# Layer 0's cross-attention: the reciprocals of the softmax sums taken one step later, behind the first four maxima of that step

## The chip, the cores and the metric

One NeuronCore of a Trainium2 chip runs the whole program. The metric is device time in microseconds (us): the kernel before takes 3111.43 us, the median of three runs that lie between 3109.09 and 3111.95. A core has five engines that work side by side, each through its own queue in order: PE (TensorE, matmuls; its weight loads are listed apart as PEld), DVE (VectorE), ACT (ScalarE), POOL (GpSimd) and SP (SyncE, which here only starts DMAs). They wait for each other through semaphores.

## The reference, cut to what matters

The program is a two-layer decoder on 32 sequences of 100 tokens with 256 channels. Each layer adds a self-attention, a cross-attention and a feed-forward block with experts. The change lies in layer 0's cross-attention, with 16 heads of 16 channels and 361 context rows per sequence:

```python
Q = (x @ Wq.T).reshape(B, xN, NUM_HEADS, HEAD_DIM)
KV = (z @ Wkv.T).reshape(B, zN, 2, NUM_HEADS, HEAD_DIM)
...
attn = jnp.einsum('bqhd,bkhd->bhqk', Q, K) * SCALE
attn = jax.nn.softmax(attn, axis=-1)
O = jnp.einsum('bhqk,bkhd->bqhd', attn, V).reshape(B, xN, DIM)
return O @ Wo.T
```

All of it is float32. A softmax needs a maximum over the 361 scores of a row, exponentials, their sum, and a division by that sum; the division is done on the output, after the product with V.

## The kernel before, in words

The function is `l0_xattn` (L513). Its work is cut into 64 units: unit M is sequence b = M // 2 and half c = M % 2 of the heads, thus 8 heads. Eight heads of 16 channels are laid on 128 partitions as four groups of 32 rows (r = 0 to 3), and each group holds two heads (j = 0 and 1), which are taken one after the other. The loop at L717 runs 66 steps; step M works on three units at once, in a software pipeline:

- `maxima(M-1)` (L618): PE turns the row maxima of the unit before (two transposes, L623), DVE adds them to the queries (L625). The tile is q2. An extra row of ones in the keys (L583) lets the next matmul subtract the maximum.
- `scores(M, j)` (L607): four matmuls with 100 queries as rows, one per group, into four PSUM banks; then four DVE maxima (L616), one per bank.
- `turned(M-1, j)` (L627): the same scores again, turned (context rows on partitions) and with the maximum subtracted: 12 matmuls into four banks, four exponentials on ACT (L637, tile e), and two additions on POOL (L641, L642, tile es), which fold the three context chunks into one, so that fewer matmuls are needed for the sum.
- `values(M-2)` (L644): 24 matmuls with V (L651) and 8 with ones (L658) into one bank, which then holds the products and the sums. ACT copies the bank to the tile zs (L663), DVE takes the reciprocal of the sums in place (L664, 128x100), POOL multiplies (L666) into zT, the input of the output projection.
- the extras of the step (L685): keys (L583) and values (L592) of the next sequence, whose PSUM banks ACT copies out (L588, L601); at every second step (c = 1) of two sequences in four also queries (L574, copies L581); at most steps with c = 0 an output projection `out_proj` (L237), whose result DVE adds to x (L243) and takes statistics of (L179, L182); and, at certain steps, pieces for the feed-forward block that follows: normalised rows on DVE (L191), their transposes (L213), and the router's logits and choice (`gates0`, L1428, with DVE's sums at L1449; `counts0`, L1453).

Inside step M the order for j = 0 is scores, turned, values, then for j = 1 scores and turned, then the extras. PE's order is exactly the written one (`manual_schedule`, L707); the queues of the other engines are ordered by the framework's scheduler.

All PSUM tiles of this function come from one ring of eight banks (`bank`, L111: every tag falls back to "t", of which there are eight). The ninth tile from any point gets the bank of the first, so a matmul waits until the reader of the tile eight places before it is done. In one step the ring is handed out as: 1 (maxima), 4 (scores j = 0), 4 (turned j = 0), 1 (values), 4 (scores j = 1), 4 (turned j = 1), then the extras, first among them the keys. Counting back eight from the keys' bank gives the first bank of scores j = 1: the keys' matmul waits for the first of the second four maxima. Counting back from turned j = 0 of the next step gives the banks of turned j = 1, of the extras and of the maxima's transposes: it waits for ACT's copies of keys, values and queries.

DVE's queue in a plain step holds: q2 (L625), four maxima of j = 0, the reciprocal of unit M-2, four maxima of j = 1.

The inner functions `scores` and `values`, and the loop that calls them, are printed here with the profile's line numbers:

Of the kernel before, what the change touches and what calls it, by code (L numbers as in the profile page):

```python
# [13 lines left out]
ALU = mybir.AluOpType  # L14
AX = mybir.AxisListType
# [66 lines left out]
class Kernel:  # L82
# [430 lines left out]
    def l0_xattn(self):  # L513
        nc, tc, a = self.nc, self.tc, self.a
        with ExitStack() as st:
# [54 lines left out]
            def load(b):  # L570
                ctx[b] = pool.tile([CD, LP], F32, tag="cT", name="cT", bufs=3)
                nc.sync.dma_start(ctx[b], a["ctxT"][:, b, :])

            def queries(b0, c):  # L574
                if c == 0:
                    q[b0 // 4] = pool.tile([P, 2, 2, 4 * T], F32, tag="qT", name="qT")
                pm = self.bank_t()[:, : 4 * T]
                self.mm(pm, [(wq[:, k, c * P : (c + 1) * P], self.xn_of(k, b0, 4)) for k in range(NK)])
                t = q[b0 // 4]
                for j in range(2):  # L580
                    nc.scalar.activation(t[:, c, j, :], pm, AF.Copy, scale=quarter[:, j : j + 1])  # L581

            def keys(b, c):  # L583
                pm = self.bank_t()[:, :L]
                self.mm(pm, [(wk[:, c * P : (c + 1) * P], ctx[b][:, :L])])
                t = ks[b % 3]
                for j in range(2):
                    nc.scalar.activation(  # L588
                        t[:, c, j, :L], pm, AF.Identity, bias=one[:, j : j + 1], scale=own[:, j : j + 1]
                    )  # L590

            def vals(b, c0, n):  # L592
                pm = self.bank_t()[:KC, : n * D].rearrange("p (c d) -> p c d", c=n)
                for i in range(n):
                    c = c0 + i
                    self.mm(pm[:, i, :], [(ctx[b][:, c * KC : (c + 1) * KC], wv)])
                pv = pm.rearrange("p c (h j d) -> p c h j d", j=2, d=16)
                v = vs[b % 3][:, c0 : c0 + n].rearrange("p c (h j) e -> p c h j e", j=2)
                for j in range(2):
                    for i in range(n):  # L600
                        nc.scalar.copy(v[:, i, :, j, 16 * j : 16 * j + 16], pv[:, i, :, j, :])  # L601

            def rows_of(r):
                return slice(32 * r, 32 * r + 32)


            def scores(M, j):  # L607
                b, c = divmod(M, 2)
                cols = slice((b % 4) * T, (b % 4 + 1) * T)
                ps = [self.bank("r")[:T, :L] for _ in range(4)]  # L610
                for r in range(4):
                    self.mm(ps[r], [(q[b // 4][rows_of(r), c, j, cols], ks[b % 3][rows_of(r), c, j, :L])])
                m = ms[M % 3]
                for r in range(4):
                    o = 32 * r + 16 * (1 - j)
                    nc.vector.tensor_reduce(m[:, j, o : o + 1], ps[r], AX.X, ALU.max, negate=True)  # L616

            def maxima(M):  # L618
                b, c = divmod(M, 2)
                cols = slice((b % 4) * T, (b % 4 + 1) * T)  # L620
                pt = self.bank_t()[:, : 2 * T].rearrange("p (j t) -> p j t", j=2)
                for j in range(2):
                    nc.tensor.transpose(pt[:, j, :], ms[M % 3][:, j, :], self.ident[:T, :T])  # L623
                q2[M] = pool.tile([P, 2, T], F32, tag="q2", name="q2")
                self.after = nc.vector.tensor_tensor(q2[M], pt, q[b // 4][:, c, :, cols], ALU.add)  # L625

            def turned(M, j):  # L627
                b, c = divmod(M, 2)
                ps = [self.bank("r")[:KC, : NKC * T] for _ in range(4)]
                for i in range(NKC):  # L630
                    for r in range(4):
                        self.mm(ps[r][:, i * T : (i + 1) * T], [(
                            ks[b % 3][rows_of(r), c, j, i * KC : (i + 1) * KC], q2[M][rows_of(r), j, :]
                        )])
                t = e[M, j] = pool.tile([KC, 4, NKC, T], F32, tag="e", name="e", bufs=5)
                for r in range(4):
                    nc.scalar.activation(t[:, r], ps[r].rearrange("p (c t) -> p c t", c=NKC), AF.Exp)  # L637

                n = L - 2 * KC
                s = es[M, j] = pool.tile([KC, 4, T], F32, tag="es", name="es", bufs=4)  # L640
                nc.gpsimd.tensor_tensor(s, t[:, :, 0, :], t[:, :, 1, :], ALU.add)  # L641
                nc.gpsimd.tensor_tensor(s[:n], s[:n], t[:n, :, 2, :], ALU.add)  # L642

            def values(M):  # L644
                b, c = divmod(M, 2)
                pz = self.bank_t()[:, : 2 * T].rearrange("p (s t) -> p s t", s=2)
                for j in range(2):
                    t = e.pop((M, j))
                    for i in range(NKC):
                        for r in range(4):  # L650
                            nc.tensor.matmul(  # L651
                                pz[rows_of(r), 0, :], lhsT=vs[b % 3][:, i, 8 * c + 2 * r + j, :],
                                rhs=t[:, r, i, :], start=(j == 0 and i == 0), stop=(j == 1 and i == NKC - 1),
                            )
                for j in range(2):
                    t = es.pop((M, j))
                    for r in range(4):
                        nc.tensor.matmul(  # L658
                            pz[rows_of(r), 1, :], lhsT=ones[:, j, :], rhs=t[:, r, :],
                            start=(j == 0), stop=(j == 1),  # L660
                        )
                zs = pool.tile([P, 2, T], F32, tag="zs", name="zs")
                nc.scalar.copy(zs, pz)  # L663
                nc.vector.reciprocal(zs[:, 1, :], zs[:, 1, :])  # L664
                for z, cols in self.z_parts(b):
                    nc.gpsimd.tensor_tensor(z[:, c, :], zs[:, 0, cols], zs[:, 1, cols], ALU.mult)  # L666

# [17 lines left out]
            def extras(b):  # L685

                k0, k1, v0, v1, o, x = [None] * 6
                if b + 1 < NB:
                    k0, k1 = (lambda: keys(b + 1, 0)), (lambda: keys(b + 1, 1))
                    v0, v1 = (lambda: vals(b + 1, 0, 2)), (lambda: vals(b + 1, 2, 1))  # L690
                if b > 1 and tile_of(b - 2) is not None:
                    o = lambda: out(tile_of(b - 2))
                b0, i = b // 4 * 4, b % 4
                if i < 2 and b0 + 4 < NB:
                    x = lambda: queries(b0 + 4, i)
                return k0, v0, o, k1, v1, x
# [11 lines left out]
            with tc.manual_schedule(engines={mybir.EngineType.PE}):  # L708
                load(0)
                load(1)  # L710
                for c in range(2):
                    queries(0, c)
                for c in range(2):
                    keys(0, c)
                vals(0, 0, 2)
                vals(0, 2, 1)
                last = 2 * NB  # L717
                for M in range(last + 2):
                    b, c = divmod(M, 2)
                    if c == 0:  # L720
                        if b + 2 < NB:
                            load(b + 2)
                        ex = extras(b)
                    if 0 < M <= last:
                        maxima(M - 1)
                    if M in norms:
                        f, *at = norms[M]
                        f(*at)
                    for j in range(2):

                        if M < last:
                            scores(M, j)
                        if 0 < M <= last:
                            turned(M - 1, j)
                        if j == 0 and M > 1:
                            values(M - 2)
                    for i in (0, 2, 1):
                        if ex[3 * c + i]:
                            ex[3 * c + i]()
                    if M not in norms or len(later) > 3:  # L740
                        for _ in range(1 + (len(later) > 3)):
                            if later:
                                later.popleft()()
                out(NF - 1)
                while later:
                    later.popleft()()
# [1335 lines left out]
```

## Time and profile before

| | |
|---|---|
| median of three runs | 3111.43 us |
| the profiled execution | 3138.55 us, span of the core 3136.8 us |
| PE busy | 3002.3 us (96%) |
| DVE busy | 1806.7 us (58%) |
| ACT busy | 1403.8 us (45%) |
| POOL busy | 911.1 us (29%) |
| mean granted TensorE clock | 0.982 of full speed |
| layer 0's cross-attention, maxima L616 first to last start | 586.5 to 1077.9 us |

The profiled execution is one run and takes 0.9% longer than the median of the unprofiled ones. Durations and waits below are from it. Busy time of PE is that of matmuls which overlap in a pipeline and whose ends are modelled, so 96% is not 96% of its peak. A line of the timeline gives the start, the length of a group of like instructions, engine, source line and operation, what is written and read with the shapes, the count, and in brackets how long the engine had been idle before it and what ended that.

### The profile page before, as it was taken

What the parts mean: (1) busy time and instruction counts of PE and PEld (TensorE: products, weight loads), DVE (VectorE), ACT (ScalarE), POOL (GpSimd) and SP (SyncE); (2) the same over time, 40 slices, a digit from 0 to 9 for tenths busy, and PEclk for the clock granted to TensorE, in tenths of its full rate; (3) what the DMA queues carried; (4) which work ended last, traced back from release to release, by engine and by line L of the source; (5) the groups of instructions that cost most, each with busy time, mean ns of one, the idle gap of its engine ahead of it and who ended that gap; (6) DMA issues with size and microseconds to landing.
All of it is one profiled execution on the core that took longest, in us unless ns stands there. A gap on an engine that the chain in (4) does not pass through costs nothing. (4 is left out here: it accounts for less than half of the span.)

```text
span 3136.8 us, 67846 instructions
## 1 busy us (share of the span) xinstructions
PE 3002.3 (96%) x26802; PEld 2251.5 (72%) x26802; DVE 1806.7 (58%) x4686; ACT 1403.8 (45%) x4361; POOL 911.1 (29%) x1040
## 2 busy tenths in 40 slices
PE   8999999999999899999998999999999999999893
PEld 7777777677777658888874677777777777776483
DVE  6666665577777632222226876666676665766354
ACT  5555554566666511122222235545555555455120
POOL 3212221465555551000015520011212112122364
PEclk9999999999999999999998999999999999999997
DMA  8860000000000033545542000010000000000296
GB/s 311 295 212 1 1 1 1 17 16 14 15 14 14 16 123 136 189 180 191 209 162 63 19 5 6 6 37 21 25 9 10 12 8 15 7 11 4 70 223 192
DMA packets 127930, 224.55 MB, mean 72 GB/s; under 512 B 39373, under 2 KB 106245, under 8 KB 120816
## 3 DMA queue, kind: packets, MB, share of 16 engines
q1 hardware_dynamic: 97680, 126.00, 12.7%
q0 software_dynamic: 26640, 90.80, 8.8%
q8 instruction: 215, 3.52, 0.5%
q10 hardware_dynamic: 3280, 3.28, 0.3%
q14 instruction: 115, 0.94, 0.1%
HBM read 152.45 MB, written 112.56 MB: 84 GB/s over the span
## 5 line engine op out<-in xcount | busy, mean ns | idle before, releaser
L1686 POOL DMA_INDIRECT x_d<-xr,slot x200 | 194.5, 972 | 773.9 <-DVE kT L133 243.6
L446 ACT ACTIVATE wBx<-ps_t,m 100x361 f32<-100x361 f32 x512 | 280.8, 560 | 258.9 <-DVE m L443 233.2
L138 PE MATMUL ps_t<-xnT,wA 128*128 128x200 f32 (+1 forms) x1600 | 328.0, 349 | 1.5 <-DMA wA<-in_wq 0.9
L138 PEld LDWEIGHTS ps_t<-xnT,wA 128*128 128x128 f32 x1600 | 271.4, 192 | 50.5 <-issue 32.2
L443 DVE TENSOR_REDUCE m<-ps_t 100x1 f32<-100x361 f32 x512 | 241.0, 525 | 78.4 <-PE ps_t L138 76.3
L138 PE MATMUL ps_t<-xT,w 128*128 128x256 f32 x1276 | 283.2, 381 | 0.7 <-ACT xT L132 0.7
L138 PEld LDWEIGHTS ps_t<-xT,w 128*128 128x128 f32 x1276 | 240.0, 190 | 41.7 <-issue 9.3
L616 DVE TENSOR_REDUCE m<-ps_t 100x1 f32<-100x361 f32 x512 | 235.4, 517 | 18.1 <-PE ps_t L138 18.1
L637 ACT ACTIVATE e<-ps_t 121x300 f32<-121x300 f32 x512 | 173.9, 426 | 123.0 <-PE ps_t L138 123.0
L340 POOL TENSOR_TENSOR e<-e,rz 100x400 f32<-100x400 f32 x128 | 109.2, 854 | 407.6 <-DVE rz L339 393.0
L336 ACT ACTIVATE e<-s,m 100x100 f32<-100x100 f32 x512 | 186.1, 365 | 21.0 <-DVE m L330 20.3
L138 PE MATMUL ps_t<-cT,wA 128*128 128x361 f32 x512 | 188.5, 492 | 1.6 <-SPq L1285 1.6
L138 PE MATMUL ps_t<-kT,qT 64*100 64x361 f32 x1024 | 189.1, 485 | 0.9 <-ACT wBx L446 0.9
L641 POOL TENSOR_TENSOR es<-e 121x400 f32<-121x400 f32 x128 | 132.2, 1033 | 197.4 <-ACT e L637 197.2
L455 PEld LDWEIGHTS ps_t<-ident,wBx 100*121 100x121 f32 x1536 | 177.9, 186 | 12.6 <-issue 5.1
L138 PE MATMUL ps_t<-wA,cT 128*121 128x512 f32 x384 | 184.9, 593 | 0.8 <-ACT wBx L446 0.8
L455 PE MATMUL ps_t<-ident,wBx 100*121 100x100 f32 x1536 | 184.8, 269 | 0.0
L138 PE MATMUL ps_t<-wA,zT 128*128 128x256 f32 x784 | 181.5, 385 | 0.0
L1367 DVE TENSOR_TENSOR h<-ps_t,g 128x256 f32<-128x256 f32 x145 | 61.2, 424 | 199.4 <-ACT g L1366 199.4
L138 PEld LDWEIGHTS ps_t<-wA,zT 128*128 128x128 f32 x784 | 147.9, 191 | 27.7 <-issue 3.3
L133 DVE COPY eT<-ps_t 121x300 f32<-121x300 f32 x339 | 146.6, 461 | 30.4 <-PE ps_t L455 26.4
L473 PE MATMUL ps_z<-eT,v 121*64 121x100 f32 x3072 | 160.9, 254 | 0.0
(317 smaller groups left out, 5741.9 us busy)
## 6 DMA issues: line engine op xcount, KB each, us to landing
x_d<-fill SPq DMA_DIRECT2D x16, 1284.0 KB
we<-in_wexp SPq DMA_DIRECT2D x32, 384.0 KB
cT<-in_ctxT SPq DMA_DIRECT2D x64, 181.5 KB
xe_d<-zero SPq DMA_DIRECT2D x8, 1024.0 KB
xe<-x_d SPq DMA_DIRECT2D x24, 321.0 KB
xe<-xe_d SPq DMA_DIRECT2D x29, 256.0 KB
y_d<-y SPq DMA_DIRECT2D x29, 256.0 KB
sum<-fill SPq DMA_DIRECT2D x10, 640.0 KB
```

The source lines that it names most:

```text
L133: return self.nc.vector.tensor_copy(out, in_)
L138: self.nc.tensor.matmul(out, lhsT=l, rhs=r, start=(i == 0), stop=(i == n - 1))
L336: nc.scalar.activation(t[:, i, :], s[:, i, :], AF.Exp, bias=m[:, i : i + 1], accum_out=rz[:, i : i + 1])
L340: nc.gpsimd.tensor_tensor(t[:, h, :], t[:, h, :], self.last(rz[:, h], T), ALU.mult)
L443: lay.after = nc.vector.tensor_reduce(m, ps[i], AX.X, ALU.max, negate=True)
L446: nc.scalar.activation(t[:, :L], ps[i], AF.Exp, bias=m, accum_out=sums[b][:, h : h + 1])
L455: nc.tensor.transpose(pt[:, c, :], e[n, i][:, c * KC : (c + 1) * KC], self.ident[:T, :T])
L473: nc.tensor.matmul(out, lhsT=v, rhs=eT[n, i][:, c, :], start=first, stop=last)
L616: nc.vector.tensor_reduce(m[:, j, o : o + 1], ps[r], AX.X, ALU.max, negate=True)
L637: nc.scalar.activation(t[:, r], ps[r].rearrange("p (c t) -> p c t", c=NKC), AF.Exp)
L641: nc.gpsimd.tensor_tensor(s, t[:, :, 0, :], t[:, :, 1, :], ALU.add)
L1686: got = nc.gpsimd.indirect_dma_start(out=self.x1_d[:, :], out_offset=bass.IndirectOffsetOnAxis(ap=slot[:, j, k : k + 1], axis=0), in_=xr[: ...
```

## The change

`values` no longer takes the reciprocal or multiplies; it returns the tile zs. A new function `divided(M, zs, after)` does both. Step M calls it for unit M-3, after the matmuls and maxima of scores j = 0, before turned j = 0. The reciprocal gets an explicit dependency on the last of these four maxima (`depend`, L1748). Step 64, which has no scores, calls it without that dependency; the last step divides units 62 and 63. The tile zs has two buffers, as before.

```diff
-                    nc.vector.tensor_reduce(m[:, j, o : o + 1], ps[r], AX.X, ALU.max, negate=True)
+                    got = nc.vector.tensor_reduce(m[:, j, o : o + 1], ps[r], AX.X, ALU.max, negate=True)
+                return got
...
                 zs = pool.tile([P, 2, T], F32, tag="zs", name="zs")
                 nc.scalar.copy(zs, pz)
-                nc.vector.reciprocal(zs[:, 1, :], zs[:, 1, :])
+                return zs
+
+            def divided(M, zs, after):
+                b, c = divmod(M, 2)
+                got = nc.vector.reciprocal(zs[:, 1, :], zs[:, 1, :])
+                if after is not None:
+                    self.depend(got, [after.ins], "behind the maxima, whose banks are waited for")
                 for z, cols in self.z_parts(b):
                     nc.gpsimd.tensor_tensor(z[:, c, :], zs[:, 0, cols], zs[:, 1, cols], ALU.mult)
...
                     for j in range(2):
 
-                        if M < last:
-                            scores(M, j)
+                        got = scores(M, j) if M < last else None
+                        if j == 0 and M > 2:
+                            divided(M - 3, zs, got)
                         if 0 < M <= last:
                             turned(M - 1, j)
                         if j == 0 and M > 1:
-                            values(M - 2)
+                            zs = values(M - 2)
+                    if M == last + 1:
+                        divided(M - 2, zs, None)
```

The order of instructions in the two built kernels differs as follows. PE, ACT and SP: not at all. DVE: in a plain step the reciprocal stands where it stood, between the two fours of maxima, but is that of unit M-3 instead of M-2, and it waits for DVE's own last maximum as well as for ACT; in steps with router work some of the small sums (L1449) stand behind it that stood ahead of it. POOL: in a step the multiplication stood between the two pairs of additions (j = 0 and j = 1); it now stands ahead of both.

## The prediction

> **What bounds the kernel now.** I read the page, then the groups by line, then the two lines of the change with what they wait for, then the timeline of every step of this stage. The page: PE is busy for 96% of the span, so only an idle PE is time to be won. The groups of the stage:
>
> ```profile
> L138 PE MATMUL ps_t<-cT,wB 128*128 128x361 f32 x124 | 54.9, 525 | 20.6 <-DVE m L616 20.6
> ...
> L664 DVE RECIPROCAL zs<-zs 128x100 f32<-128x100 f32 x64 | 49.7, 776 | 64.8 <-ACT zs L663 64.8
> ```
>
> PE stands idle for 20.6 us ahead of the keys' matmuls, which wait for a maximum; that is nearly all its recorded idle time here. DVE stands idle for 64.8 us ahead of its reciprocals. How the two hang together, in one plain step with an output projection (the timeline from 656 to 674 us):
>
> ```profile
> 659.76 0.87 PE L138 MATMUL ps_t<-k,qT 32*100 32x361 f32 x8
> 659.94 0.33 ACT L663 COPY zs<-ps_t 128x200 f32<-128x200 f32 x1 [0.34 <-issue]
> ...
> 660.30 0.78 DVE L664 RECIPROCAL zs<-zs 128x100 f32<-128x100 f32 x1 [1.07 <-ACT zs L663]
> 660.45 0.79 PE L138 MATMUL ps_t<-q,k 32*121 32x100 f32 x24
> ...
> 660.99 1.79 DVE L616 TENSOR_REDUCE m<-ps_t 100x1 f32<-100x361 f32 x4
> ...
> 661.52 0.88 PE L138 MATMUL ps_t<-cT,wB 128*128 128x361 f32 x2 [0.28 <-DVE m L616]
> ...
> 664.16 0.77 ACT L601 COPY v<-ps_t 121x128 f32<-121x128 f32 x4 [0.47 <-PE ps_t L138]
> ...
> 664.91 0.94 PE L138 MATMUL ps_t<-q,k 32*121 32x100 f32 x24
> 665.11 1.85 DVE L616 TENSOR_REDUCE m<-ps_t 100x1 f32<-100x361 f32 x4 [0.41 <-PE ps_t L138]
> ```
>
> The reciprocal is queued ahead of the second four maxima and waits for ACT's copy. So the maxima start at 660.99, the first (about 0.52 us) ends at 661.51, and at 661.52 PE may write the keys into the bank it read. PE had finished at 661.24: 0.28 us idle. This repeats in almost every step.
>
> **The change, part by part.**
>
> *The reciprocal.* Its data are now a step old, so it runs right behind the first four maxima. The four before this step's reciprocal start at 657.38 and take 1.85 us, to 659.23; a reciprocal of 0.78 ends at 660.01, in time in which DVE was idle for 1.07. The added wait, for DVE's own last maximum, costs about 0.1 us (like instructions overlap by 0.07 us; the statistics, which wait for DVE's own addition, start 0.04 us after its end), inside the same idle time.
>
> *The second maxima.* The first four start 0.89 us after their scores (664.22 to 665.11). So the second can start at 659.76 + 0.89 = 660.65 instead of 660.99, 0.34 earlier, and the keys at 661.18. Could PE go that early? Behind the j = 0 matmuls it goes on 0.06 us before their modelled end (664.91 + 0.94 = 665.85, next at 665.79), here 661.18. So 0.34 us per step; the recorded idle time gives the lower bound, 0.28.
>
> *What is late next.* Turned j = 0 of the next step waits for ACT's copies. Above, the values' copies wait 0.47 for PE; if PE comes 0.34 earlier, they do too. There the whole 0.34 counts. Not so here:
>
> ```profile
> 668.79 1.36 ACT L637 ACTIVATE e<-ps_t 121x300 f32<-121x300 f32 x4 [0.99 <-PE ps_t L138]
> ...
> 670.01 1.22 ACT L588 ACTIVATE k<-ps_t,one,own 128x361 f32<-128x361 f32 x2
> ...
> 671.31 1.08 ACT L581 ACTIVATE qT<-ps_t,quarter 128x400 f32<-128x400 f32 x2
> ...
> 672.28 0.43 ACT L601 COPY v<-ps_t 121x128 f32<-121x128 f32 x2
> ...
> 672.40 1.07 PEld L138 LDWEIGHTS ps_t<-q,k 32*121 32x121 f32 x24 [0.33 <-ACT qT L581]
> ```
>
> With queries ACT works from its exponentials to the last copy with 0.08 us of rest (671.23 to 671.31): only that can be won, and PE then waits for ACT. I sorted the steps by this: 22 with an output projection have ACT's pause of 0.46 to 0.50; 10 more are set by PE or by a DVE copy behind PE (transposes copied by DVE, router matmuls). 32 x 0.34 = 10.9 us. Six with queries: 6 x 0.08 = 0.5. In the rest ACT has no pause, or they are router steps: 0 from this part.
>
> *The multiplications.* The same 112 on POOL (0.31 us each), now ahead of the first additions. These could start at 659.68; now the reciprocal ends at 660.01 and one multiplication takes 0.40, so they start at about 660.45, 0.77 later, and end (2 x 1.07) at 662.59. The second pair starts at 662.69 in any case: a margin of 0.1. PE needs the sums at 666.84, long after. The output projection gets its input earlier than now.
>
> *The lock between DVE and POOL.* In a router step (the timeline from 819 to 823 us):
>
> ```profile
> 819.82 1.09 DVE L1449 TENSOR_TENSOR acc<-acc,sel 128x8 f32<-128x8 f32 x2
> ...
> 819.85 1.03 POOL L641 TENSOR_TENSOR es<-e 121x400 f32<-121x400 f32 x1 [2.40 <-ACT e L637]
> ...
> 820.83 0.77 DVE L664 RECIPROCAL zs<-zs 128x100 f32<-128x100 f32 x1
> ...
> 822.04 0.88 PE L138 MATMUL ps_t<-cT,wB 128*128 128x361 f32 x2 [0.61 <-DVE m L616]
> ```
>
> The second 8-column sum takes 0.90 us, not 0.15: it ends when POOL's addition does. The reciprocal took 0.78 beside POOL all through. The Trainium skill ("SBUF — State Buffer", "Who interferes with whom") has the rule behind it: DVE and GpSimd share one pair of SBUF ports; a DVE operation with two SBUF inputs, or in a 2-port mode (`tensor_scalar` can be), blocks for the whole of a GpSimd operation that came first; reductions and one-input operations do not. By the rule alone the change looks bad, since POOL's run moves towards the next step's norm rows (L191). By the rows the cost is: 1.13 instead of 0.40 us for a norm row that met POOL at 1046.69, thus up to 0.73 where they meet. The trace shows both signs:
> - For: in a router step POOL now starts only after the reciprocal, so the sums run free, 0.75 us sooner. Most of these steps then meet ACT, whose pause is 0.28: two at 0.28; the step at 882 (locked twice, PE idle 1.79) 1.2; that at 1008 0.8. Together 2.6.
> - Against: where norm rows follow such a step, POOL's run ends later and they wait: at 762 about 0.85, at 1064 0.5, at 794 and 921 0.15, at 613 and 672 0.1. Together 1.9.
>
> Net +0.7; kept for the range: +4.0 (nothing against) to -3.7 (twice against, nothing for).
>
> *Sum.* 10.9 + 0.5 + 0.7 = 12.1 us. Against the profiled execution: 3138.55 - 12.1 = 3126.5, its span 3136.8 to 3124.7. That execution is 0.9% longer than the median; the stage's clock is granted at 1.00 in most windows, so I carry the 12 us over unscaled: 3111.4 - 12 = 3099.5. Bounds: 32 x 0.28 + 0 - 3.7 = 5.3, and 10.9 + 0.5 + 4.0 = 15.4, thus 3096 to 3106. The feed-forward block begins behind the last step's chain, so I take none of it back.
>
> **The rivals.**
>
> *ACT takes it all but in steps that PE sets without a projection.* If ACT's exponentials or key copies run later than the timeline lets me see, its pause of 0.47 is not free to give: only 10 x 0.34 = 3.4 us, 3108. For: ACT has no pause in about 20 steps. Against: the 0.46 is there in 22 steps. Chance 0.15.
>
> *Slower: POOL's run reaches the next step.* Place: the second pair of additions. If the multiplication delays it by over 0.5 us in every step (the margin is 0.1, so this decides from a reciprocal that ends about 0.6 us later than I put it, or slower POOL operations), POOL holds the ports when 15 steps' norm rows (15 x 0.73 = 11) and ten router steps' two-input operations (10 x 0.9 = 9) begin. 20 - 12 = +8: 3119. For: the rows at 762 and 1046 already suffer it. Against: in plain steps the first pair still ends before the second can start. Chance 0.09.
>
> *It does nothing.* The keys wait for a maximum whichever is ahead of it; if DVE's wake-up for the second four is 0.34 us longer than for the first, nothing is gained: 3111. Against: 0.89 in step after step. Chance 0.07.
>
> *The lock's relief passes to PE in full*: 3095 or less. Chance 0.08.
>
> **How the numbers follow.** The forecast keeps 0.61. A measurement of this kernel can tell about 0.2% (6.2 us) from no change, so faster means below 3105.2: the forecast but for its upper edge (0.58), the lock's relief (0.08), and the luckier part of the first rival (0.05): 0.71. Slower: POOL's run, and a little of "nothing" (0.10). Same: 0.19. The range, 3095 to 3109, holds the forecast with its bounds and the first rival; it leaves out the slower case, most of "nothing" and the far side of the relief.
>
> **What would show it.** Right: idle time ahead of the reciprocals near 0 instead of 64.8; ahead of the keys' matmuls 20.6 down to under 5; steps with a projection 7.54 us long now (from the first V matmul to that of the next step), 7.20 then; those with queries, 7.78, nearly as now, with turned j = 0 waiting for ACT; the sums L1449 at 0.15. Wrong: new idle time of PE ahead of L651 or turned j = 0 in all steps (ACT), norm rows of over 1 us in most of their steps (POOL), or keys that still wait.

## The result and the profile after

The changed kernel takes 3095.02 us, the median of four runs (3094.41 to 3096.36), beside 3110.26 us for the kernel before on the same chip (3108.37 to 3111.95, four runs). The ratio is 0.9951, with a 95% interval of 0.994 to 0.9963: 15.2 us less, with 11.5 to 18.7 us in the interval. The forecast was 3099.5 us, 12 us less. The profiled execution takes 3096.36 us, its span is 3094.6 us, and its granted clock 0.986.

First the groups of the stage after the change, in the part of the profile that lists instructions by line. A row has the busy time, the mean of one in ns, and behind the second bar the engine's idle time ahead of it with what ended it.

```profile
L652 PE MATMUL ps_t<-e,v 121*32 121x100 f32 x3072 | 81.0, 255 | 5.7 <-DVE m L616 5.6
...
L138 PE MATMUL ps_t<-cT,wB 128*128 128x361 f32 x124 | 54.2, 519 | 0.4 <-DVE m L616 0.4
...
L669 DVE RECIPROCAL zs<-zs 128x100 f32<-128x100 f32 x64 | 49.8, 778 | 11.4 <-ACT zs L664 5.9
...
L673 POOL TENSOR_TENSOR zT<-zs 128x100 f32<-128x100 f32 (+24 forms) x112 | 32.2, 306 | 162.3 <-DVE zs L669 129.0 <-DVE acc L1459 27.5 <-DVE pr L1473 3.9
...
L191 DVE TENSOR_SCALAR wAn<-x_sb,mv,rstd 128x256 f32<-128x256 f32 x23 | 14.0, 639 | 0.3
...
L1459 DVE TENSOR_TENSOR acc<-acc,sel 128x8 f32<-128x8 f32 x20 | 2.8, 138 | 0.1
```

Three of these rows as they were before:

```profile
L651 PE MATMUL ps_t<-e,v 121*32 121x100 f32 x3072 | 80.2, 253 | 3.0 <-DVE m L616 3.0
...
L191 DVE TENSOR_SCALAR wAn<-x_sb,mv,rstd 128x256 f32<-128x256 f32 x23 | 10.7, 495 | 0.3
...
L1449 DVE TENSOR_TENSOR acc<-acc,sel 128x8 f32<-128x8 f32 x20 | 9.8, 492 | 0.3
```

The reciprocals still cost 778 ns each, but the 64.8 us of DVE's idle time ahead of them are down to 11.4. Of these, 5.9 are three waits for ACT from 1061 us on, at the end of the stage. PE's 20.6 us ahead of the keys are down to 0.4. Two rows went the other way: the norm rows are slower (a mean of 639 ns, before 495), and PE waits 5.6 us for a maximum ahead of the V matmuls (L652), before 3.0. The router's sums went from a mean of 492 ns to 138.

One plain moment in the timeline after, which answers to the one shown of before:

```profile
665.09 0.78 DVE L669 RECIPROCAL zs<-zs 128x100 f32<-128x100 f32 x1
665.32 0.87 PE L138 MATMUL ps_t<-k,qT 32*100 32x361 f32 x8
665.50 0.33 ACT L664 COPY zs<-ps_t 128x200 f32<-128x200 f32 x1 [0.34 <-issue]
...
666.01 0.79 PE L138 MATMUL ps_t<-q,k 32*121 32x100 f32 x24
666.21 1.86 DVE L616 TENSOR_REDUCE m<-ps_t 100x1 f32<-100x361 f32 x4 [0.34 <-PE ps_t L138]
...
666.79 0.30 PEld L138 LDWEIGHTS ps_t<-cT,wB 128*128 128x128 f32 x2 [0.16 <-DVE m L616]
666.79 0.88 PE L138 MATMUL ps_t<-cT,wB 128*128 128x361 f32 x2
```

The reciprocal starts (665.09) before ACT has even begun this step's copy (665.50): it works on the unit before. DVE then waits for PE, not ACT, and the second maxima start 0.89 us after their scores (665.32 to 666.21), where it was 1.23 (659.76 to 660.99). PE passes from turned j = 1 to the keys without a gap. POOL's multiplications, which had waited 3.3 us in the whole stage for the reciprocals, now wait 129.0 us, and the additions stand behind them.

To see where the time came from, I measured each step from its first V matmul to that of the next, and added the steps up by kind. The comparison is with a second record of the same instruction order as before (the sixth experiment below). From the first scores to the last matmul with ones that record has 502.10 us and the kernel after 489.28: 12.8 us less. The rest of the 15.2 lies within the interval of the ratio.

| kind of step (number) | predicted, us | after | sums first | no reciprocal | rows late |
|---|---|---|---|---|---|
| with an output projection (24), or set by PE or a DVE copy (7) | -10.9 (for 32) | -9.0 | -8.6 | -9.0 | -10.4 |
| with queries (7) | -0.5 (for 6) | -1.1 | -1.2 | -1.3 | -1.3 |
| no pause of ACT (9) | 0 | -0.1 | 0.0 | 0.0 | -0.1 |
| with a load of ACT's tables (3) | 0 | -1.2 | -0.2 | -1.0 | -1.2 |
| router (4) | -2.6 | -2.4 | -1.5 | -1.5 | -3.2 |
| other steps with norm rows or router work (7) | +1.9 (for 6) | +1.0 | -2.1 | -2.6 | -4.6 |
| the last two | 0 | 0.0 | -0.1 | -1.6 | +0.2 |
| sum of steps 2 to 64 | -12.1 | -12.8 | -13.6 | -17.0 | -20.4 |

The three columns on the right are experiments. Of the prediction's six steps with a loss by norm rows, two (at 613 and 672) are among those with queries. The entries of the last two kinds must be read with care: in some of these records the clock was granted at 0.50 for 3.4 us or more in such steps, and in others it was not. That is worth 0.5 to 1.5 us; the fifth experiment shows it.

### The profile page after: what moved, and what is told of

Same layout as the page of the kernel before. It is cut to its first block, busy times and chain, and to the rows that moved or that the text cites. A ratio compares the mean times of both kernels' runs of the same rounds, so it can differ in the third digit from the quotient of the medians.

```text
span 3094.6 us, 67901 instructions
## 1 busy us (share of the span) xinstructions
PE 2990.6 (97%) x26802; PEld 2248.3 (73%) x26802; DVE 1813.6 (59%) x4686; ACT 1400.7 (45%) x4361; POOL 910.9 (29%) x1040
## 3 DMA queue, kind: packets, MB, share of 16 engines
q1 hardware_dynamic: 97680, 126.00, 12.8%
## 5 line engine op out<-in xcount | busy, mean ns | idle before, releaser
L138 PEld LDWEIGHTS ps_t<-cT,wA 128*128 128x128 f32 x512 | 87.0, 189 | 97.4 <-issue 54.1
```

What stands on the lines that cost most here:

```text
L138: self.nc.tensor.matmul(out, lhsT=l, rhs=r, start=(i == 0), stop=(i == n - 1))
```

## The experiments

My theory: the gain is the wait for ACT taken out from ahead of the second maxima; the lock between DVE and POOL gives and takes about as much. Rivals: POOL's new order makes the gain; the place within the step makes it, not the age of the data; or DVE's lighter load would do it.

**1. The multiplications called later** (`e1_product_between`): they are taken out of `divided` into a function `product`.

```diff
                             turned(M - 1, j)
+                        if j == 0 and M > 2:
+                            product(M - 3, zs)
```

> The changed kernel, but POOL's multiplications stand between the two pairs of additions again; the reciprocal stays a step later. Theory (the removed wait of VectorE is the gain, POOL's new order only a small net): the 32 steps set by PE keep their 0.29 us, the router steps lose what they won by an idle POOL (some 4 us), the norm rows behind them lose less (some 2 us): 3097 us, idle time ahead of the keys near 1 us in plain steps. Rival (POOL's order is the main source): 3105 to 3110 us.

Measured: 3095.09 us, ratio 0.995 (0.9936 to 0.9963). POOL's waits and the router's sums (138 ns) are those of the kernel after. The orders of both engines in the built kernel say why: they are the same, instruction for instruction, as after. The framework's scheduler puts the multiplication ahead of the additions wherever the call stands. So this is a repeat of the kernel after and decides nothing; experiment 5 puts it right with an explicit dependency.

**2. The same step's reciprocal, behind the second maxima** (`e2_same_step_last`): the wait for ACT moves to a place where the copy is long done.

```diff
-                        if j == 0 and M > 2:
-                            divided(M - 3, zs, got)
...
-                    if M == last + 1:
-                        divided(M - 2, zs, None)
+                    if M > 1:
+                        divided(M - 2, zs, got)
```

> The reciprocal of the same step's unit, put behind the second four maxima instead of a step later. It waits for nobody there either, and the keys' bank is free as early. Theory (the place behind the first four is what costs nothing, since VectorE rests there; behind the second four come the projection's addition, its statistics and q2, on the way to PE's next matmuls): the 22 steps with a projection give back about 0.3 us each: some 6 to 7 us, so 3101 us. Rival (only the wait ahead of the second maxima counts, the place of the reciprocal does not): 3095 us, like the changed kernel.

Measured: 3106.16 us, ratio 0.9992 (0.9984 to 1.0001): hardly a gain, and both expectations missed. Its groups:

```profile
L138 PE MATMUL ps_t<-q,k 32*121 32x100 f32 x3048 | 129.4, 272 | 4.7 <-DVE q L626 3.0 <-ACT v L601 1.0 <-DVE m L616 0.2
L652 PE MATMUL ps_t<-e,v 121*32 121x100 f32 x3000 | 77.9, 252 | 9.2 <-DVE m L616 8.8
...
L191 DVE TENSOR_SCALAR wAn<-x_sb,mv,rstd 128x256 f32<-128x256 f32 x23 | 16.7, 753 | 0.3
```

The keys are freed (PE waits 1.2 us for them in the stage), and most steps with a projection win 0.23 us, nearly the 0.29 of the change. So these plain steps give back 0.05 us, not 0.3 as I had expected; the loss sits in steps with norm rows or router work. There q2 now waits for the reciprocal ahead of it, and PE for q2 (3.0 us in the stage). And the norm rows follow the reciprocal closely, while POOL is in its run: 753 ns each, and PE waits 8.8 us behind them. Taking the data a step later is therefore part of the gain against this place: it lets the reciprocal stand where nothing waits for DVE. POOL has its old order here: its multiplications wait 99.0 us for the reciprocals in the stage, and the second pair of additions stands behind them. How much of the loss comes from this, and how much from the place in DVE's queue, is not told apart; no other place was tried.

**3. No reciprocal at all** (`e3_no_reciprocal`), made from the kernel before; it leaves out the division.

```diff
-                nc.vector.reciprocal(zs[:, 1, :], zs[:, 1, :])
```

> The kernel before without the reciprocal: the output of the attention is multiplied by the sum instead of divided by it. Theory (the wait is the cost, and 0.78 us of VectorE matter only in the router steps): the plain steps become as short as in the changed kernel (7.25 with a projection, 7.59 with queries), the router steps win up to 0.78 each by less work: 3094 us, range 3092 to 3097. Rival (VectorE's own time is the bound in most steps): clearly below the changed kernel, 3085 us.

Measured: 3093.08 us, ratio 0.9943 (0.993 to 0.9957), within the expectation. Plain steps with a projection are 7.25 us long, exactly as after: the moved reciprocal costs nothing there. That DVE's load of 50 us costs anything is not shown. Against experiment 5, which has the reciprocals, this kernel wins 0.8 us in the steps with table loads, but in these POOL's multiplication stands one addition sooner. It wins 0.5 in the seven other steps and 1.5 in the last two, but there the clock was lower in the record of experiment 5. In nearly all other steps POOL has its old order here, and the router's sums are still slow (510 ns), and yet the router steps win 1.5 us.

**4. Norm rows behind the first four maxima** (`e4_norm_rows_late`), on the kernel after.

```diff
-                    if M in norms:
-                        f, *at = norms[M]
-                        f(*at)
                     for j in range(2):

                         got = scores(M, j) if M < last else None
+                        if j == 0 and M in norms:
+                            self.after = got or self.after
+                            f, *at = norms[M]
+                            f(*at)
```

> The changed kernel with the norm rows of a step behind its first four maxima instead of ahead of them. Theory (what the changed kernel still loses to the lock sits in norm rows that wait for POOL and hold the first maxima, thus the V matmuls: 5.6 us of PE's idle time in 7 steps): POOL rests while the rows run there, so they take 0.4 us each; PE's idle time ahead of the V matmuls falls below 1 us: 3091 us. Rival (the rows then hold the reciprocal and the second maxima as long, and POOL's run starts later still): no gain, 3095 us.

Measured: 3086.18 us, ratio 0.9923 (0.9909 to 0.9936), and once more on another chip (`e10_rows_late_again`):

> The kernel with the norm rows behind the first four maxima once more, beside the one above on the same chip: ratio 0.9923 (0.991 to 0.9936) as measured before. If its gain over the changed kernel was the chip's, 0.995.

There 3089.87 us, ratio 0.9935 (0.9921 to 0.9949). It beats both kernels, by some 5 to 9 us against the change. The stage is 481.63 and 481.83 us long in the two records and 489.28 in the kernel after, so about 7.5 us shorter; 1.5 of this lie in two steps in which the clock of the kernel after was low (the fifth experiment). PE's idle time behind a maximum ahead of the V matmuls falls from 5.6 us to 0. What happens is best seen in one place. In the kernel after, at the start of step 24:

```profile
756.69 2.38 DVE L191 TENSOR_SCALAR wAn<-x_sb,mv,rstd 128x256 f32<-128x256 f32 x2
...
756.79 1.03 POOL L642 TENSOR_TENSOR es<-e 121x400 f32<-121x400 f32 x1
...
757.89 1.03 POOL L643 TENSOR_TENSOR es<-es,e 119x400 f32<-119x400 f32 x1
...
759.57 1.15 PE L652 MATMUL ps_t<-e,v 121*32 121x100 f32 x44 [1.24 <-DVE m L616]
```

And with the rows late:

```profile
756.27 1.03 POOL L643 TENSOR_TENSOR es<-es,e 119x400 f32<-119x400 f32 x1
...
756.62 1.24 PE L652 MATMUL ps_t<-e,v 121*32 121x100 f32 x48
757.32 0.74 DVE L191 TENSOR_SCALAR wAn<-x_sb,mv,rstd 128x256 f32<-128x256 f32 x2
```

Beside POOL two rows took 2.38 us, to 759.07, a little beyond the end of POOL's second addition at 758.92; after POOL was done, at 757.30, they took 0.74. In their old place the maxima stand behind them, and PE behind these for 1.24 us.

**5. The kernel after with POOL's old order** (`e5_sums_first`): each multiplication depends explicitly on the first pair of additions.

```diff
+                    got = nc.gpsimd.tensor_tensor(z[:, c, :], zs[:, 0, cols], zs[:, 1, cols], ALU.mult)
+                    if after is not None:
+                        self.depend(got, [after.ins], "behind the first pair of additions")
```

> The kernel after, with POOL's multiplications bound behind the first pair of additions, POOL's order of before; DVE's order is that of after. What falls away is only the later start of POOL's additions. The prediction's account (POOL's new order is a small net gain: router sums run free, some norm rows wait): the router sums go back from 0.14 to about 0.49 us, the two router steps lose their 0.39 again, and the time is 3096 (3095 to 3098). Rival (the steps with norm rows and the tail lose more by the new order than the router steps win): norm rows fall from 0.64 and 0.51 us to about 0.50 and 0.41, the kernel without a reciprocal, which has POOL's old order, is the model with 3093.1, and this one lands at 3093 (3091 to 3094.5). Plain steps 7.25 in both.

Measured: 3121.01 us where the kernel before takes 3136.24 on that chip; ratio 0.9952 (0.9938 to 0.9967), the same as after. The two forecasts, 3093 and 3096, give ratios of 0.9945 and 0.9954 with the 3110.26 above, which the interval holds both, so the time doesn't decide. The norm rows take 568 ns in the mean (tile wAn) and 491 (tile xn), between those of before (495 and 409) and after (639 and 510). The row of the router's sums:

```profile
L1467 DVE TENSOR_TENSOR acc<-acc,sel 128x8 f32<-128x8 f32 x20 | 4.9, 245 | 0.1
```

The sums do not fall back to 0.49 us, as I had expected, but to 0.245. The timeline of a router step in this kernel tells why:

```profile
813.96 0.16 DVE L1467 TENSOR_TENSOR acc<-acc,sel 128x8 f32<-128x8 f32 x1
813.97 1.04 POOL L642 TENSOR_TENSOR es<-e 121x400 f32<-121x400 f32 x1 [2.07 <-ACT e L638]
814.14 0.78 DVE L669 RECIPROCAL zs<-zs 128x100 f32<-128x100 f32 x1
814.84 0.20 DVE L1467 TENSOR_TENSOR acc<-acc,sel 128x8 f32<-128x8 f32 x1
```

POOL's addition starts at the same point as in the kernel before, just after the first sum has begun. But the reciprocal, which no longer waits for ACT, now stands between the two sums. It runs beside POOL, and when the second sum comes up at 814.84, less than 0.2 us of POOL's addition are left (it ends at 815.01). Before, the second sum took 0.90 us and the reciprocal came after it.

By steps, POOL's new order wins 0.9 us in the router steps (all in that at 994) and 1.0 in those with a load of tables, and it loses 3.0 in the seven steps below them in the table. With small differences elsewhere it costs 0.8 us in the sum of the steps. But not all of this is POOL's order. Here are two matmul groups of the kernel after, around 1043 us, and then the same two in this kernel:

```profile
1042.16 1.42 PE L138 MATMUL ps_t<-q,k 32*121 32x100 f32 x24
1043.51 2.04 PE L652 MATMUL ps_t<-e,v 121*32 121x100 f32 x48
```

```profile
1043.65 0.83 PE L138 MATMUL ps_t<-q,k 32*121 32x100 f32 x24
1044.44 1.24 PE L652 MATMUL ps_t<-e,v 121*32 121x100 f32 x48
```

The matmuls themselves are slower in the kernel after. The view by windows gives the reason; its columns are the window, its length, the busy time of PE, PEld, DVE, ACT and POOL, the granted clock, and DMA. The kernel after, then this one:

```profile
1041.80:1045.20 3.40, 3.40 (x76) 3.13 (x72) 3.24 (x16) 1.36 (x4) 0.00 (x0) 0.50 0.00 0
```

```profile
1043.50:1046.90 3.40, 3.40 (x114) 3.06 (x110) 3.37 (x17) 1.68 (x5) 0.94 (x1) 1.00 0.02 5
```

The clock was at 0.50 there, and the two steps that share this stretch are 0.73 and 0.81 us longer than in this kernel. The record of experiment 1, with the same order as after, has the stretch too. In this kernel's own record the clock is at 0.50 from 1019.0 to 1022.4, and the two steps there are 0.23 and 0.30 us longer than after. Of the 3.0 us, then, only 2.0 (three steps, 0.65 to 0.70 each) come at the same clock. Without the four disturbed steps POOL's new order wins 0.2 us in place of the loss of 0.8, and the lasting result is that it is worth less than 1 us either way.

**6. The kernel after without the named wait** (`e6_no_named_wait`).

```diff
-                            divided(M - 3, zs, got)
+                            divided(M - 3, zs, None)
```

> The kernel after without the named wait of the reciprocal for the last of the first four maxima; in the order of DVE it moves in two places only. Prediction's account: that wait of about 0.1 us lies inside DVE's idle time, so the time stays: 3095 (3094 to 3096), plain steps 7.25, DVE's idle time ahead of the reciprocals as now. Rival (the wait is paid on the path to the second maxima): 30 steps by up to 0.1, 3092.

Measured: 3136.65 us, ratio 1.0003 (0.9994 to 1.0012): the whole gain is gone. Both expectations were wrong, and so was my reading of the order: each step has one reciprocal, and all of them had moved by a step. Against the kernel before there is no difference on DVE or POOL: without the dependency the scheduler put the reciprocal back in the old place. The groups of this kernel:

```profile
L138 PE MATMUL ps_t<-cT,wB 128*128 128x361 f32 x124 | 54.2, 519 | 20.6 <-DVE m L616 20.6
L669 DVE RECIPROCAL zs<-zs 128x100 f32<-128x100 f32 x64 | 49.7, 776 | 65.1 <-ACT zs L664 65.1
```

They are those of before. So the price of the wait itself was not tested; what was shown is that it holds the reciprocal in its place, and that the later call alone changes nothing. As a second record of the old order this run is worth more: its steps agree with the first record within 0.02 us in all but two places. Step 39 is one. The columns are those of the windows above. Before, then this record:

```profile
884.00:889.00 5.00, 3.56 (x14) 2.67 (x18) 3.02 (x8) 2.38 (x7) 2.69 (x4) 0.66 0.03 4
```

```profile
884.00:889.00 5.00, 3.21 (x44) 2.45 (x42) 4.49 (x11) 2.81 (x8) 3.13 (x4) 1.00 0.14 38
```

In the first record the granted clock was 0.66 in the mean of these 5 us (0.50 for 3.4 of them), and the step lasted 1.55 us longer. Against it, this step would seem to win 2.22 us by the change; against the second it is 0.67. At the tail the difference has the other sign, 1.0 us. That is why the table uses the second record.

**7. Less work for ACT** (`e7_half_value_copies`): half of the values' copies are left out.

```diff
-                for j in range(2):
-                    for i in range(n):
-                        nc.scalar.copy(v[:, i, :, j, 16 * j : 16 * j + 16], pv[:, i, :, j, :])
+                for i in range(n):
+                    nc.scalar.copy(v[:, i, :, 0, 0:16], pv[:, i, :, 0, :])
```

> The kernel after, leaving out half of ACT's copies of the values in this stage (the odd heads' columns stay zero), so that ACT has 0.2 to 0.4 us less to do in every step with values. Theory (ACT sets only the nine steps that gained nothing, and the query steps, and in the plain steps PE and the maxima set the length): plain steps stay at 7.25, the nine gain up to 0.3 each (2.7 in all), the query steps about 0.1 each (1.2 in all): 3091 (3089.5 to 3093). Rival (with the keys 0.29 earlier ACT sets the plain steps as well, so ACT is the reason that they gained 0.29 and not 0.34): they fall to 7.20, 32 by 0.05, and if ACT alone sets them to 7.1 or less: 3087 or lower. If ACT's copies are not on the path at all: 3095.

Measured: 3115.07 us beside 3136.24, ratio 0.994 (0.9923 to 0.9956). Steps with a projection stay at 7.25 (-7.2 us in their sum, after -7.0); the nine steps win 2.4 us, those with queries 0.9 more than after, those with table loads 1.1 more. The row of turned in this kernel:

```profile
L138 PE MATMUL ps_t<-q,k 32*121 32x100 f32 x3072 | 124.0, 269 | 1.8 <-DVE q L625 1.5
```

In the kernel after, PE waits 3.0 us there, 1.9 of them for ACT's copies of the values; that wait is gone. ACT does set the nine steps and those with queries, and not the plain ones.

**8. Norm rows late without the change** (`e8_rows_late_alone`): experiment 4's edit on the kernel before.

> The kernel before with the norm rows placed behind the first four maxima, and the reciprocal where it was. Theory (the rows' late place is a gain of its own only where PE waited for a maximum behind them, 3.0 us in before; the rest of its 8.9 us belongs to the change, which makes POOL's run later and lets the rows hide where DVE used to wait): 3106.5 (3105 to 3108). Rival (the gain is independent of the change): 3101.3 (3100 to 3103). If the rows push the reciprocal and with it the second maxima later by more than they win: 3110 or more.

Measured: 3137.74 us, ratio 1.0008 (0.9998 to 1.0018). My theory had 3 to 4 us of gain here; there is none, and the third outcome comes nearest. In the timeline at 1008:

```profile
1007.91 1.03 POOL L642 TENSOR_TENSOR es<-e 121x400 f32<-121x400 f32 x1 [3.24 <-ACT e L638]
1007.99 1.09 DVE L191 TENSOR_SCALAR wAn<-x_sb,mv,rstd 128x256 f32<-128x256 f32 x1
...
1009.08 1.12 DVE L191 TENSOR_SCALAR wAn<-x_sb,mv,rstd 128x256 f32<-128x256 f32 x1
...
1011.34 0.97 PE L138 MATMUL ps_t<-cT,wB 128*128 128x361 f32 x2 [1.86 <-DVE m L616]
```

With POOL's old order the first additions begin just where the rows now stand, and the keys wait 1.86 us behind them. The keys' row of the stage, which had 20.6 us in the old order:

```profile
L138 PE MATMUL ps_t<-cT,wB 128*128 128x361 f32 x124 | 54.3, 520 | 25.3 <-DVE m L616 25.1
```

PE's wait ahead of the V matmuls is gone here too (from 2.9 us to 0), but the keys' wait grew by 4.5. In experiment 4 POOL has to wait for the reciprocal behind the rows, so that place is free of it. The stage is 3.4 us longer than in the old order. This record also has three stretches of 3.4 us with the clock at 0.50 (from 1012, 1039 and 1060) that the other lacks; at half speed each can cost at most 1.7 us, so without them the rows alone would win 1.7 us at the most (an estimate). The 7.5 us that the rows win in experiment 4 thus need the change: one made the room for the other. That it is POOL's order which makes the room, and not the maxima's freedom from ACT, is read from the timelines; late rows with POOL's old order and the moved reciprocal were not run.

**9. Values' copies shared with DVE** (`e9_rows_late_values_shared`), on top of experiment 4, to use what experiment 7 had found.

```diff
+                        copy = nc.vector.tensor_copy if split and j else nc.scalar.copy
+                        copy(v[:, i, :, j, 16 * j : 16 * j + 16], pv[:, i, :, j, :])
```

> The kernel with the norm rows behind the first four maxima (ratio 0.9923), and in addition half of the values' copies given to DVE in the steps where ACT is found to be the limit: even steps without an output projection, and all odd steps. Theory (ACT sets those steps; leaving half the copies out won 2.4 us in the nine that ACT sets, 0.9 in those with queries, 1.1 where exponentials' tables are loaded): DVE has the time to take them before it adds q2, so some 3 to 4 us of this come, ratio 0.991 (0.990 to 0.992). Rival (the copies delay q2 or the first maxima on DVE, 0.2 us each in 32 steps): 0.9923 or more, PE's idle time behind DVE up from 0.6 us ahead of turned j = 0.

Measured: 3097.67 us, ratio 0.9966 (0.9952 to 0.9979), slower than with the rows alone. The groups show the rival:

```profile
L138 PE MATMUL ps_t<-q,k 32*121 32x100 f32 x3072 | 132.3, 271 | 8.8 <-DVE q L627 4.0 <-DVE v L602 3.0 <-DVE m L617 1.0
```

DVE's copies wait 10.0 us for ACT's copies of the same tile, q2 waits behind them, and PE for both.

## Why the prediction was right, and where its terms were off

*What bounds the kernel.* One reading was too strong: the waits listed for PE in this stage before add up to 29.7 us, so the keys' 20.6 are two thirds of them, not nearly all. It does not touch the sum, which was made from the steps.

*The reciprocal.* Right. It is back in the idle time behind the first maxima, and without it (experiment 3) plain steps are no shorter. Whether the added wait costs 0.1 us stays open, as experiment 6 didn't have the order that it needed.

*The second maxima.* The mechanism is right, the size was 0.29 us and not 0.34. The maxima do start 0.89 us after their scores, 0.34 sooner. But I let PE go on 0.06 before the modelled end of turned j = 1, as it does behind j = 0; the lines after show the keys at 666.79, and 666.01 + 0.79 is 666.80. Their weight load starts at that same moment and had waited 0.16 for a maximum. The lower bound of 0.28, read from the recorded idle time, was the better number: 31 steps gained 9.0 us and not 10.9 (which was for 32).

*What is late next.* The sorting held: the nine steps in which ACT has no pause gained 0.1 us together, and experiment 7 shows that ACT sets them. Five of the query steps gained 0.19 to 0.21 each and not 0.08; the two ahead of the norm rows at 613 and 672 gained 0.07 and 0.08, and so fell short of the others by about the 0.1 us that I had set against them. Here ACT's own lines after:

```profile
668.04 1.22 ACT L588 ACTIVATE k<-ps_t,one,own 128x361 f32<-128x361 f32 x2
...
669.11 1.11 ACT L581 ACTIVATE qT<-ps_t,quarter 128x400 f32<-128x400 f32 x2
```

The keys' copies end at 669.26 and the queries' start at 669.11: back to back, one starts 0.15 before the other's recorded end. So the pause of 0.08 that I read from ends and starts was probably larger by about this much (the Trainium skill, in "ScalarE: Activation LUTs", "What ACT_TABLE_LOAD costs", puts the overlap of such instructions at about 93 ns; here it is 0.15 us). I had no term for the steps with a load of ACT's tables, which gained 1.2 us. Before, the keys wait for a maximum in them as in the plain steps (0.33 us at 729.73), and the change takes that away. In experiment 5, which frees the keys too, most of this gain is lost again: the multiplication stands ahead of POOL's last additions, two norm rows take 1.08 us beside these, and PE waits 0.26 for the maxima behind them. In the kernel before and in that after the two rows take 0.73 and 0.74.

*The multiplications.* Right: PE's wait for them ahead of the output projection is 1.1 us in the stage, and the second pair of additions is not delayed enough to reach every step. The rival that said so was wrong in its extent: it wanted 15 steps with rows and ten router steps, and the seven other steps with norm rows or router work lost 1.0 us in all, less than the low clock took in two of them (1.5).

*The lock between DVE and POOL.* This step of the sum was right only in part. Router steps won 2.4 us where I had 2.6, but the cause was in the main another: 1.5 of it come with POOL in its old order too. In experiment 5 the reciprocal fills the time in which the second sum would wait; in experiment 3 the sum waits as before, but no reciprocal follows it. In the step at 882 the gain was 0.67 and not 1.2: PE's old wait of 1.79 is down to 0.35, but the norm rows of the next step take 1.51 us beside POOL, and PE waits 0.96 behind them. Against experiment 5 three row steps lose 2.0 us at the same clock: that ahead of the rows at 762 0.70, where I had 0.85, and those at 794 and 921 about 0.66 each instead of 0.15. The other 1.0 of the 3.0 us there lies in the four steps in which the clock was low in one of the two records, and can't be put down to the lock. So POOL's later start, which I counted as +0.7, lies between +0.2 and -0.8; what the router steps won without it, by the reciprocal between the sums, made up for that. The range's +4.0 also doesn't follow from my own terms: with nothing against, they give 2.6, and a bound of 3097 instead of 3096. As the Trainium skill has it ("SBUF — State Buffer", "Who interferes with whom"), the waiting operation is held for the whole of POOL's; two rows of 2.38 us beside two additions, and of 0.74 once they are done, agree with that rule, and experiment 4 shows what it was worth.

*Sum.* 12.1 against 12.8 in the stage: too high by 1.9 in the plain steps, too low by 1.8 in those with queries and table loads, and too high a loss by 0.9 in the steps with norm rows. The low clock around 1043 took back about 1.5 us that I had not forecast. That the total fits so well is in part luck.

## What to carry to other kernels

An operation that waits for another engine should not stand ahead of one that frees a buffer; give it data that are a step old, and tie it explicitly to its place, since here the scheduler put it straight back without the tie. Price the gain by the idle time that is recorded at the waiting engine, not by how much earlier its releaser starts. And when two engines exclude each other, look at which of their operations now meet: here the second gain, of about 7.5 us in the stage, came from moving the norm rows into the gap that the first had opened, and was worth nothing without it.

## What the runs showed of the hardware

- A granted clock of 0.50 for 3.4 us in one record of the same instruction order made one step 1.55 us longer, and the same in the kernel after made two steps 1.5 us longer than in experiment 5. Why the clock falls was not tested. A comparison by steps needs two records and the granted clock of each step, or it finds causes that are not there.
- One chip ran the kernel before in 3136.24 us (experiments 5 to 8); in the other measurements it took 3109 to 3110. The granted clocks are 0.979 to 0.983 in the runs on the first and 0.983 to 0.987 in the others. The ratios are not hurt by it: the order of before gave 1.0003 there.
- Copies that follow each other on ACT overlap by 0.15 us in the records, so a pause read between two of them can be that much too short.
